# A four-layer graph network on one core: twenty mask pieces set earlier, and the first two weights of a unit made by the unit before it

## The chip, the cores and the metric

The kernel runs on one core of a Trainium2 chip. The metric is the device time of one execution in microseconds (us). The kernel before the change takes 3250.54 us, the median of three runs (3249.86 to 3252.36). Engines are called by their short names: PE (TensorE, matmuls; PEld is its loading of stationary operands), DVE (VectorE), ACT (ScalarE), POOL (GpSimd) and SP (SyncE, which here only issues transfers).

## The reference

The input is `x` (3327 x 512, float32) and an adjacency matrix `adj` (3327 x 3327, int32, zeros and ones). Four layers follow one another, and each is added to its input and normalised along the row:

```python
x = layernorm(x + gat(x, adj, W0, a0))            # layer 0, 8 heads
x = layernorm(x + sage(x, adj, ...))              # layer 1, first 64 neighbours of each row
x = layernorm(x + elu(gat(x, adj, W2, a2)))       # layer 2, 8 heads
x = layernorm(x + elu(gat(x, adj, W3, a3)))       # layer 3, 4 heads

def gat(x, adj, W, a):                            # per head
    h = x @ W
    e = leaky_relu((h @ a1)[:, None] + (h @ a2)[None, :], 0.2)
    return softmax(where(adj > 0, e, -9e15), axis=1) @ h
```

What matters here is that each attention layer needs, for every head, a 3327 x 3327 matrix of weights that are zero wherever `adj` is zero, and that the first layer has to read all of `adj` (4 bytes an element) before that is known on the chip.

## The kernel before

**Tiles and halves.** The rows are padded to 3328 = 26 tiles of 128 (`NT` = 26). A half of the rows is 13 tiles or 1664 columns (`HALF`, `IW`). The transposed adjacency matrix is turned once into a mask of ones and zeros in fp8, `mask0[p, t, i]`: tile `t` holds 128 neighbours, `i` runs over all 3328 rows. It is made in pieces `(t, q)`, `t` a tile and `q` a quarter of the columns (832): a load of int32 values, 416 KB, into a tile `raw` (L884, issued by SP), and a set, one instruction that compares it with zero, on DVE (L895) or on ACT (L894). Quarters 0 and 1 are the first half of the rows, 2 and 3 the second. That makes 104 pieces.

**The first projection** (the loop `for t in range(1, NT)` around L1443) takes one tile of `x` a turn: `project1` transposes it (PE L267, copy on ACT L268, a sum over it on DVE L269), `project2` of the tile before multiplies it by the weights (16 matmuls, PE L277) and scales the result on DVE (`vt`, L283), which POOL stores (L289). Two or three steps of `msteps` are written into each turn. A step `k` loads piece `k` and sets piece `k - 5`; there are eight `raw` tiles. Here the list has the 52 pieces of the first half. Late in the loop POOL also loads the row values of the first unit (`wide_rows`, `rba`, 2 x 832 KB).

**The attention of layers 0 and 2** (`attention8`, `unit8`) runs eight units of 26 tiles `j`. The units numbered 0 and 7 treat two heads over one half of the rows, and the six between treat one head over all rows. For each tile, DVE makes the weights `t` (L702, one pass over 3328 columns, or two over 1664), ACT turns them into the fp8 selector `y` (L703), and PE multiplies `t` with the values (L724, 16 instructions) and `y` with the pieces of the denominator (L680). There are three `t` tiles, so DVE can be up to three tiles ahead of PE. At the end of each turn one entry is taken from two lists: `background` (among it `count_jobs`, which on PE counts the mask's ones over all 26 tiles, L925) and `aside`. In layer 0 `aside` holds the other 52 mask pieces (`some`, four steps in three turns); here a step loads piece `k` and sets piece `k - 1`, there are two `raw` tiles, four in nine sets go to ACT, and each set is pinned.

**The attention of layer 3** (`attention`, `unit`) runs eight units as well: two halves of the rows by four heads `s`. For tile `j`, `weights(j, k)` issues the pass on DVE (L428) and the one on ACT (L431), PE multiplies (L451) and adds up the denominator (`den`, L403). At the end of a unit the four accumulators `po` are emptied into `ob`: in the first half by four DVE transposes (L470), in the second by a DVE copy (L474) and three ACT copies (L472). Where a denominator is complete, DVE also transposes it (L521, L525), reduces it (L529), and POOL spreads it over the partitions (L541). The next unit's first matmul must wait for `ob`, since it uses the same accumulators. `rows` (L372, POOL) loads the row values of a unit into one of two slots. In the second half of the rows, `aside` holds the finishing of the first half: loads, division by the denominator (L182), exponential (L189), sums (L197, L198), normalisation (L153 to L162) and stores.

**Order.** On PE the order is that of the program text (`tc.manual_schedule`). On the other engines a planner lays out each queue when the program is built: it plays the program through with its own durations, and an instruction that is ready in that play may stand ahead of earlier written ones. `tc.keep_in_program_order(ins)` ties an instruction behind the one written just before it on its engine ("pinned"). Each engine then works through its queue strictly in order, so one that waits holds up everything behind it.

Of the kernel before, what the change touches and what calls it, by code (L numbers as in the profile page):

```python
# [13 lines left out]
ALU = mybir.AluOpType  # L14
# [18 lines left out]
def kernel(  # L33
# [10 lines left out]
    nc = tc.nc  # L44
    N, F = x.shape
    NT = (N + P - 1) // P
# [3 lines left out]
    NS = F // P  # L50
    HALF = NT // 2
    FW = F // 2
    assert F == 512 and NT % 2 == 0 and N < NP and NT < 32
    IW = HALF * P
# [2 lines left out]
    CUTS = ((0, WA // 2), (WA // 2, WA), (WA, WA + WB // 2), (WA + WB // 2, IW))  # L57
    assert WA // 2 <= 512
    PIECES = (0, 48, 72, 32)
    QUADS = [(s, min(4, HALF - s)) for s in range(0, HALF, 4)]  # L60


# [55 lines left out]
    mask_at = []  # L118
# [113 lines left out]
    class Layer:  # L232
# [151 lines left out]
                                                                     u.half * IW:(u.half + 1) * IW].to_broadcast([P, IW]))  # L384
            return r_

        def unit(self, pools, half, s, background, aside, final=None, ending=None):
            H, D, HS = self.H, self.D, self.HS
            tp, yp, vp, rp, sp, po_p = pools
            i0 = half * IW  # L390
            heads = list(range(s * HS, (s + 1) * HS))
            rb, self.first_rows = self.first_rows or self.rows(rp, half, s), None
            po = [po_p.tile([P, 512], F32, name=f"po{c}") for c in range(4)]
            if s == 0:
                self.pd = [po_p.tile([P, 512], F32, name=f"pd{c}") for c in range(2)]
# [26 lines left out]
                       ys[j][k][:, a_:a_ + w_], w_,  # L422
                       s == NS - 1 or final is not None and s > 0)

            def weights(j, k):
                h = heads[k]
                t = tp.tile([P, IW], F32, name="t")
                nc.vector.scalar_tensor_tensor(t, rb[k], self.qc[:, j, h:h + 1],  # L428
                                               mask_at[0](j, i0, IW), op0=ALU.max, op1=ALU.mult)
                y = yp.tile([P, IW], F8, name="y")  # L430
                nc.scalar.activation(y, t, AF.Sigmoid, bias=self.bi[:, j, h:h + 1],  # L431
                                     scale=self.sc[:, j, h:h + 1], saturate=False)
                return t, y

            late = []
            for j in range(NT):
                if j % 2 == 0:
                    vj = vp.tile([P, 2, P], F32, name="vj")
                    nc.sync.dma_start(out=vj, in_=self.vd[j * P:(j + 2) * P, s * P:(s + 1) * P]
                                      .rearrange("(t p) f -> p t f", p=P))  # L440


                if HS == 1 or j not in (1, NT - 1):
                    made = {}
                    for k in range(HS):
                        for j_ in (j, j + 1) if HS > 1 and j in (0, NT - 2) else (j,):
                            made[j_, k] = weights(j_, k)
                ts, ys = zip(*(made[j, k] for k in range(HS)))
                for c, (a_, z) in enumerate(CUTS):
                    for k in range(HS):  # L450
                        nc.tensor.matmul(po[c][k * D:(k + 1) * D, :z - a_], vj[:, j % 2, k * D:(k + 1) * D],  # L451
                                         ts[k][:, a_:z], start=j == 0, stop=j == NT - 1)
                late.append(ys)
                if j % 4 == 0 and j > 0:
                    for j_ in (j - 4, j - 2):
                        den(j_, [late.pop(0), late.pop(0)])
                if background:
                    background.pop(0)()
                if aside:
                    aside.pop(0)()  # L460
            if ending:
                ending(sp)
            den(NT - 2, late)

            ob = sp.tile([P, IW], F32, name="ob", bufs=1)
            by_dma = HS == 1 and not final
            for c, (a_, z) in enumerate(CUTS):
                if by_dma:

                    nc.vector.transpose(ob[:, a_:z], po[c][:, :z - a_])  # L470
                elif c or HS == 2:
                    nc.scalar.copy(ob[:, a_:z], po[c][:, :z - a_])  # L472
                else:
                    nc.vector.tensor_copy(ob[:, a_:z], po[c][:, :z - a_])  # L474
            t0 = half * HALF

            def transposed(s0, n):
# [38 lines left out]
            if not by_pe:  # L516
# [2 lines left out]
                end = half == 1 and s == NS - 1  # L519
                for c in range(2):  # L520
                    ins = nc.vector.transpose(db[:64, c * (WA // 2):(c + 1) * (WA // 2)], pd[c][:64, :WA // 2])  # L521
                    if end and c == 0:

                        tc.keep_in_program_order(ins)
                    nc.vector.transpose(db[64:, c * (WB // 2):(c + 1) * (WB // 2)], pd[c][64:, :WB // 2])  # L525
                red = yp.tile([P, WA // 32, 2, NS], F32, name="red", tag="y")
                dv = db.rearrange("p (b s x) -> p b s x", s=NS, x=8)
# [88 lines left out]
        def attention(self, rp, extra=None, aside=(), later=None, final=None, ending=None):  # L616
            with tc.tile_pool(name="at_t", bufs=3 * self.HS, reuse_waits="tile") as tp, \
                    tc.tile_pool(name="at_y", bufs=7, reuse_waits="tile") as yp, \
                    tc.tile_pool(name="at_v", bufs=3, reuse_waits="tile") as vp, \
                    tc.tile_pool(name="at_s", bufs=2, reuse_waits="tile") as sp, \  # L620
                    tc.tile_pool(name="at_po", bufs=1, space=PSUM, reuse_waits="tile") as po_p:
                pools = (tp, yp, vp, rp, sp, po_p)
                jobs = []
                aside = list(aside)
                for half in range(2):
                    for s in range(NS):
                        if extra:
                            jobs += extra(sp, half, s)
                        if later and half == 1:
                            aside += later(s)  # L630
                        jobs += self.unit(pools, half, s, jobs, aside, final if half else None,
                                          ending if (half, s) == (1, NS - 1) else None)
                while jobs:
                    jobs.pop(0)()
                for f in aside:
                    f()
# [310 lines left out]
    class MaskTiles:  # L947
# [6 lines left out]
        def start(self):  # L954
            self.early = self.pools.enter_context(tc.tile_pool(name="mk_a", bufs=1, side="right", reuse_waits="tile"))
            self.tiles = {j: self.early.tile([P, NP], F8, name=f"mk{j}") for j in range(self.FIRST)}
# [435 lines left out]
    with tc.tile_pool(name="mask0", bufs=1, reuse_waits="tile") as mp0, \  # L1392
# [8 lines left out]
        with tc.tile_pool(name="p_w", bufs=1, reuse_waits="tile") as wp, \  # L1401
# [3 lines left out]
            if LAST < P:  # L1405
                nc.gpsimd.memset(mask0[:, NT - 1, :], 0.0)
            nc.gpsimd.memset(mask0[:, :, N:NP], 0.0)
            pieces = [(t, q, IW // 2) for t in range(NT) for q in range(2)]
            msteps = mask_steps(rw0, pieces, 5, (), False, 8)

            def load(t):
# [31 lines left out]
            for t in range(1, NT):  # L1443
                xT = L0.project1(pp, ps, load(t), t)
                L0.project2(pp, bank, wsb, *pend)
                pend = (xT, t)
                for _ in range(2 + (t % 3 == 1)):
                    if msteps:
                        msteps.pop(0)()
                if t == HALF + 1:  # L1450
                    L0.prepare(pp, 0)
                    L0.cut(pp, 0)
                if t == NT - 6:
                    L0.first_rows = L0.wide_rows(ring, UNITS[0])
# [22 lines left out]
            return []  # L1477


        pieces = [(t, q, IW // 2) for t in range(NT) for q in range(2, 4)]  # L1480
        rest = ExitStack()
        rawp = rest.enter_context(tc.tile_pool(name="raw", bufs=2))
        ring.insert(0, (rest.enter_context(tc.tile_pool(name="at_s0", bufs=1, reuse_waits="tile")), "rbb"))
# [86 lines left out]
```

## Time and profile before

| what | value |
| --- | --- |
| median of three runs | 3250.54 us |
| the profiled execution | 3248.35 us, of it the span of the engines' work 3246.5 us |
| PE busy | 3135.6 us (97%) |
| DVE, ACT busy | 2623.7 us (81%), 2293.6 us (71%) |
| first projection and what leads to it, to the first weights on DVE | 0 to 133.77 us |
| layer 0's attention, first to last of its matmuls' copies | 135.7 to 954.4 us |
| layer 3's attention, first matmul to last | 2555.9 to 3217.4 us |
| mask sets on DVE | 81, median 593 ns, the last at 319.4 us |
| mask sets on ACT | 23, median 988 ns, the last at 319.1 us |

PE is busy in nearly all of the span, so what counts is where PE stands still, or runs at less than its full clock, and what it then waits for. A timeline lists instructions in order of time: start, duration, engine, line, operation, tiles, and in brackets the idle time of that engine just before, with what ended it. The table of windows gives, for stretches of time, each engine's busy time with the number of instructions, the granted PE clock (1.00 is full), the DMA engines' share and what they moved.

### The profile page before, as it was taken

Reading aid. Unit: us, or ns where it says so; the run is one execution under the profiler, and the core shown is the slowest. Engines: PE = TensorE matmul, PEld = TensorE weight load, DVE = VectorE, ACT = ScalarE, POOL = GpSimd, SP = SyncE. Lnnn points to the kernel's source line nnn. Section 1 sums busy time; section 2 is a strip of 40 time slices with the busy share of each in tenths; the row PEclk is TensorE's granted clock in tenths of the full one; section 3 lists DMA queues with packets and bytes.
Section 4 is the critical chain, followed back from the end, with each engine's and each line's share of the span. In section 5 each row is a group of like instructions: output and inputs, shape, how many; then the busy total and the mean of one; then the engine's idle time right before and its main releaser. Section 6 shows DMA issues by size and latency. Waiting matters only on the chain. (4 is left out here: it accounts for less than half of the span.)

```text
span 3246.5 us, 44851 instructions
## 1 busy us (share of the span) xinstructions
PE 3135.6 (97%) x17910; PEld 1599.6 (49%) x17910; DVE 2623.7 (81%) x2320; ACT 2293.6 (71%) x1826; POOL 231.8 (7%) x378
## 2 busy tenths in 40 slices
PE   8998999999999999999989999999988999999997
PEld 7643343333334467777733333333337655555453
DVE  5698999999987645555499999999989666677887
ACT  2498888899873334444388988899988655568886
POOL 3100000000010111111100000000001000010110
PEclk9999999999999999999999999999999999999998
DMA  9554114111134345555331111011137211122211
GB/s 366 171 175 145 41 52 145 51 42 41 29 99 131 99 134 130 139 141 146 105 122 55 41 35 41 21 41 42 28 100 238 96 42 43 44 56 89 88 42 52
DMA packets 354575, 300.07 MB, mean 92 GB/s; under 512 B 232420, under 2 KB 288174, under 8 KB 352831
## 3 DMA queue, kind: packets, MB, share of 16 engines
q1 hardware_dynamic: 322175, 185.92, 19.9%
q0 software_dynamic: 26672, 103.60, 10.2%
q10 hardware_dynamic: 5520, 7.69, 0.7%
q8 instruction: 141, 2.31, 0.3%
q14 instruction: 67, 0.55, 0.1%
HBM read 220.27 MB, written 76.84 MB: 92 GB/s over the span
## 5 line engine op out<-in xcount | busy, mean ns | idle before, releaser
L703 ACT ACTIVATE y<-t,bi,sc 128x3328 fp8e4<-128x3328 f32 (+1 forms) x520 | 1337.3, 2603 | 109.2 <-DVE t L702 51.4
L724 PE MATMUL po<-t,vj 128*64 128x448 f32 (+1 forms) x6656 | 1278.4, 525 | 16.6 <-DVE t L702 15.6
L724 PEld LDWEIGHTS po<-t,vj 128*64 128x64 f32 x6656 | 459.0, 138 | 703.4 <-issue 632.3
L451 PE MATMUL po<-t,vj 128*128 128x448 f32 (+1 forms) x1664 | 599.4, 517 | 5.6 <-DVE t L428 3.5
L428 DVE SCALAR_TENSOR_TENSOR t<-rba,qc,mk 128x1664 f32<-128x1664 f32 x208 | 404.1, 1947 | 141.2 <-PE po L451 109.6
L431 ACT ACTIVATE y<-t,bi,sc 128x1664 fp8e4<-128x1664 f32 x208 | 365.6, 1772 | 184.4 <-DVE t L428 167.7
L451 PEld LDWEIGHTS po<-t,vj 128*128 128x128 f32 x1664 | 311.5, 190 | 274.1 <-issue 170.9
L702 DVE SCALAR_TENSOR_TENSOR t<-rba,qc,mk 128x3328 f32<-128x3328 f32 (+1 forms) x130 | 379.6, 2986 | 11.8 <-DMA mk<-md 7.8
L702 DVE SCALAR_TENSOR_TENSOR t<-rbb,qc,mask 128x3328 f32<-128x3328 f32 (+1 forms) x130 | 380.3, 2981 | 9.1 <-PE po L724 6.2
L702 DVE SCALAR_TENSOR_TENSOR t<-rbb,qc,mk 128x3328 f32<-128x3328 f32 (+1 forms) x130 | 379.2, 2985 | 8.7 <-PE po L724 6.7
L702 DVE SCALAR_TENSOR_TENSOR t<-rba,qc,mask 128x3328 f32<-128x3328 f32 (+1 forms) x130 | 380.5, 2981 | 6.7 <-PE po L724 5.9
L1164 PE MATMUL acc<-zs,kt 128*128 128x512 f32 x1352 | 360.2, 420 | 0.0
L277 PE MATMUL pw<-wsb,xT 128*128 128x264 f32 (+1 forms) x1248 | 297.7, 393 | 6.3 <-DVE vt L283 3.5
L1164 PEld LDWEIGHTS acc<-zs,kt 128*128 128x128 f32 x1352 | 255.6, 189 | 52.1 <-PE pk L1015 0.8
L680 PE MATMUL pd<-y,sden 128*32 128x384 fp8e4 (+1 forms) x3328 | 271.2, 344 | 0.0
L277 PEld LDWEIGHTS pw<-wsb,xT 128*128 128x128 f32 x1248 | 238.9, 195 | 49.2 <-ACT xT L268 5.2
L1022 ACT CAST pk<-cy 128x512 f32<-128x512 bf16 x169 | 99.1, 587 | 222.4 <-DVE kt L1036 215.9
L1036 DVE SCALAR_TENSOR_TENSOR kt<-pk,mb 128x512 fp32r<-128x512 f32 x169 | 115.4, 684 | 116.7 <-PE pk L1033 115.5
L680 PEld LDWEIGHTS <-sden 128*32 128x32 bf16 x3328 | 89.5, 95 | 165.8 <-issue 150.2
L283 DVE TENSOR_TENSOR vt<-pw,dc 128x256 f32<-128x256 f32 x156 | 59.1, 418 | 90.6 <-ACT dc L278 84.6
L1062 PE MATMUL pz<-wn,xT 128*128 128x512 f32 x208 | 96.0, 605 | 6.1 <-DMA wn<-in_wnT_dram 5.4
L992 POOL DMA_DIRECT2D cy<-ctd x91 | 67.9, 746 | 366.9 <-ACT pk L1022 301.2
(221 smaller groups left out, 2079.3 us busy)
## 6 DMA issues: line engine op xcount, KB each, us to landing
raw<-in_adjT_dram SPq DMA_DIRECT2D x67, 416.0 KB
vj<-v SPq DMA_DIRECT2D x156, 128.0 KB
cy<-ctd POOLq DMA_DIRECT2D x78, 256.0 KB, 4.3
h<-hd SPq DMA_DIRECT2D x61, 256.0 KB
v<-vt SPq DMA_DIRECT2D x50, 256.0 KB
xr<-x POOLq DMA_DIRECT2D x45, 256.0 KB, 3.4
md<-mask SPq DMA_DIRECT2D x26, 416.0 KB
mb<-md SPq DMA_DIRECT2D x169, 64.0 KB
```

The source lines that it names most:

```text
L277: nc.tensor.matmul(pw[e][:, :FW + H], xT[:, c, :], wsb[:, c, e, :], start=c == 0, stop=c == FC - 1)
L428: nc.vector.scalar_tensor_tensor(t, rb[k], self.qc[:, j, h:h + 1], mask_at[0](j, i0, IW), op0=ALU.max, op1=ALU.mult)
L431: nc.scalar.activation(y, t, AF.Sigmoid, bias=self.bi[:, j, h:h + 1], scale=self.sc[:, j, h:h + 1], saturate=False)
L451: nc.tensor.matmul(po[c][k * D:(k + 1) * D, :z - a_], vj[:, j % 2, k * D:(k + 1) * D], ts[k][:, a_:z], start=j == 0, stop=j == NT - 1)
L680: nc.tensor.matmul(pd[c][32 * kk:32 * kk + 32, :w_], lhsT, rhs, start=(kk, c) not in seen, stop=last and j == NT - 1)
L702: nc.vector.scalar_tensor_tensor(to, ro, self.qc[:, j, h:h + 1], m, op0=ALU.max, op1=ALU.mult)
L703: nc.scalar.activation(yo, to, AF.Sigmoid, bias=self.bi[:, j, h:h + 1], scale=self.sc[:, j, h:h + 1], saturate=False)
L724: nc.tensor.matmul(po[c][k * D:(k + 1) * D, :z - a_], vj[:, j % 2, x_:x_ + D], t[:, k, a_:z], start=j == 0, stop=j == NT - 1)
L1022: nc.scalar.copy(pks[k % 2], carry[b, t // 4 * 4][:, t % 4:t % 4 + 2, :])
L1036: nc.vector.scalar_tensor_tensor(kt, pk, NEIGHBOURS, mb[:, t:t + 2, :], op0=ALU.is_le, op1=ALU.mult)
L1062: nc.tensor.matmul(pz, xT[:, c, :], wn[:, c, :], start=c == 0, stop=c == FC - 1)
L1164: nc.tensor.matmul(acc, kts[b, t][:, s * P:(s + 1) * P], zs(t, c), start=t == 0 and c == 0, stop=t == NT - 1 and c == 1)
```

## The change

It has two parts. First, the ten tiles 0 to 9 of the second half of the rows (`EARLY` = 10, quarters 2 and 3, twenty pieces) move from layer 0's attention to the end of the projection's list. That list grows from 52 to 72 pieces, and its steps from 57 to 77; the turns 22 to 25 of the projection now hold seven steps each in place of two or three. The list in the attention shrinks from 52 to 32 pieces (33 steps in place of 53); at four steps in three turns it ends in unit 0, where before it ran on into unit 1.

Second, in layer 3 a unit knows its follower (`following`). At tile 13 it loads the follower's row values. After its last tile it makes the follower's weights of tile 0 (`start(0)`), and, after emptying the accumulators, those of tile 1 (`start(1)`); both DVE passes are pinned. The follower takes them from `self.started`. All transposes of the first part of the denominator on DVE are pinned now, where only one was.

```diff
+    EARLY = 10
...
-            def weights(j, k):
-                h = heads[k]
+            def weights(j, k, rb=rb, h0=heads[0], i0=i0, pinned=False):
+                h = h0 + k
                 t = tp.tile([P, IW], F32, name="t")
-                nc.vector.scalar_tensor_tensor(t, rb[k], self.qc[:, j, h:h + 1],
-                                               mask_at[0](j, i0, IW), op0=ALU.max, op1=ALU.mult)
+                ins = nc.vector.scalar_tensor_tensor(t, rb[k], self.qc[:, j, h:h + 1],
+                                                     mask_at[0](j, i0, IW), op0=ALU.max, op1=ALU.mult)
+                if pinned:
+                    tc.keep_in_program_order(ins)
...
+                ts, ys = zip(*([started.pop(j)] if j in started else [weights(j, k) for k in range(HS)]))
+                if following and j == HALF:
+                    self.first_rows = self.rows(rp, *following)
...
             if ending:
                 ending(sp)
+
+            def start(j):
+                if following:
+                    self.started[j] = weights(j, 0, self.first_rows, following[1], following[0] * IW, True)
+
+            start(0)
             den(NT - 2, late)
 
             ob = sp.tile([P, IW], F32, name="ob", bufs=1)
...
                 else:
                     nc.vector.tensor_copy(ob[:, a_:z], po[c][:, :z - a_])
+            start(1)
             t0 = half * HALF
...
                     ins = nc.vector.transpose(db[:64, c * (WA // 2):(c + 1) * (WA // 2)], pd[c][:64, :WA // 2])
-                    if end and c == 0:
-
-                        tc.keep_in_program_order(ins)
+                    tc.keep_in_program_order(ins)
...
-            pieces = [(t, q, IW // 2) for t in range(NT) for q in range(2)]
+            pieces = [(t, q, IW // 2) for t in range(NT) for q in range(2)] + \
+                [(t, q, IW // 2) for t in range(EARLY) for q in range(2, 4)]
             msteps = mask_steps(rw0, pieces, 5, (), False, 8)
...
                 pend = (xT, t)
-                for _ in range(2 + (t % 3 == 1)):
+                for _ in range(2 + (t % 3 == 1) if t < NT - 4 else 7):
                     if msteps:
                         msteps.pop(0)()
...
-        pieces = [(t, q, IW // 2) for t in range(NT) for q in range(2, 4)]
+        pieces = [(t, q, IW // 2) for t in range(EARLY, NT) for q in range(2, 4)]
```

## The prediction, made before the change was run

> **What bounds the kernel now.** I read the page's busy shares first: PE 97%, DVE 81%, ACT 71%. The kernel can gain only where PE stands still or runs slowly, so the next view was PE's timeline, searched for idle times above 0.25 us, and then the DVE's and ACT's timelines at those places. The chain that ended last covers only the tail after 3138 us and says nothing on these stages.
>
> The stage that loses mask sets is layer 0's unit 1, some 254 to 371 us. PE, then DVE, then ACT:
>
> ```profile
> 254.41 3.16 PE L724 MATMUL po<-t,vj 128*64 128x448 f32 x16
> 260.48 4.71 PE L724 MATMUL po<-t,vj 128*64 128x448 f32 x16 [2.91 <-DVE t L702]
> 310.78 3.02 PE L724 MATMUL po<-t,vj 128*64 128x448 f32 x16 [0.82 <-DVE t L702]
> 320.10 0.59 PE L925 MATMUL pct<-mask,onecol 128*32 128x512 fp8e4 x1 [4.15 <-ACT mask L894]
> 320.61 5.66 PE L724 MATMUL po<-t,vj 128*64 128x448 f32 x16
> ...
> 256.24 0.60 DVE L895 TENSOR_SCALAR mask<-raw 128x831 fp8e4<-128x831 int32 x1 [4.29 <-DMA raw<-in_adjT_dram]
> ...
> 319.07 0.97 ACT L894 ACTIVATE mask<-raw,below 127x832 fp8e4<-127x832 int32 x1
> ```
>
> Three idle times of PE come from mask pieces. The set at 256.24 waits 4.29 us for its load and holds up the weights behind it; 0.82 us goes the same way; at 320.10 the count over all 26 tiles waits 4.15 us for the last set. After the long ones the same 16 matmuls take 4.71 and 5.66 us where 3.01 is usual.
>
> The stage that takes over the twenty pieces:
>
> ```profile
> 69.98 3.80 PE L277 MATMUL pw<-wsb,xT 128*128 128x264 f32 x16 [0.20 <-DVE vt L283]
> 74.42 3.80 PE L277 MATMUL pw<-wsb,xT 128*128 128x264 f32 x16 [0.20 <-DVE vt L283]
> ...
> 118.43 3.73 PE L277 MATMUL pw<-wsb,xT 128*128 128x264 f32 x16
> ...
> 60.00:70.00 10.00, 9.42 (x48) 7.54 (x46) 6.99 (x15) 2.54 (x12) 2.15 (x4) 1.00 1.03 407
> ...
> 110.00:120.00 10.00, 10.00 (x53) 8.64 (x52) 4.33 (x9) 2.79 (x11) 1.62 (x3) 1.00 0.14 53
> ```
>
> Up to 95 us, where the last of the 52 sets runs, transfers fill the DMA engines (407 GB/s) and a tile takes 4.43 us, with three sets on DVE in it; after that PE sets a pace of 4.00 us, and DMA and DVE have room.
>
> The stage of the second part, layer 3, is full of PE at seven boundaries of units but for two:
>
> ```profile
> 2967.57 0.69 DVE L182 TENSOR_TENSOR h<-h,rec 128x512 f32<-128x512 f32 x1 [4.10 <-DMA h<-hd]
> 2968.29 0.62 DVE L474 COPY ob<-po 128x448 f32<-128x448 f32 x1
> 2968.97 8.65 PE L451 MATMUL po<-t,vj 128*128 128x448 f32 x24 [2.08 <-DVE ob L474]
> ...
> 3051.08 0.62 DVE L521 STREAM_TRANSPOSE db<-pd 64x448 f32<-64x448 f32 x1
> 3051.72 0.59 DVE L525 STREAM_TRANSPOSE db<-pd 64x384 f32<-64x384 f32 x1
> 3056.59 10.34 PE L451 MATMUL po<-t,vj 128*128 128x448 f32 x24 [3.51 <-DVE t L428]
> ```
>
> At 2966.9 us the copy that frees an accumulator stands behind a division whose load is late. At 3053.1 us the second weight of the new unit is made only after the denominator's transposes.
>
> **What the Trainium skill says.** "TensorE: Matmul & The Clock Gate", part 1, "What's actually happening": after an idle window of about 3.4 us the array's clock falls to half, and about as long of work brings it back. The windows agree: granted clock 0.50 from 320.6 to 323.0 us and 0.59 from 260.5 to 264.0; even the 2.91 us gap brought it on, while those of 0.82 and 1.23 us were followed by matmuls of the usual length. "DMA: Bandwidth & Descriptors", "Where 436 GB/s comes from": a ceiling of 435 GB/s, with the memory's share of about 358 binding first. Here the plateau is 405 to 411 GB/s, so the measurement decides. "Perfetto Trace Analysis", "Identifying the Most-Contended Engine": matmul busy time is no measure of PE's room[...]. The 97% agrees with that: it includes the slow matmuls above.
>
> **Part one, what it removes.** The list of 33 steps ends in turn 24 of unit 0, as four steps go in three turns. Unit 0 keeps the same density of sets, so nothing changes there. In unit 1 all sets go: the three gaps, 2.91 + 0.82 + 4.15 = 7.88 us, and the slow matmuls after them, (4.71 - 3.01) + (5.66 - 3.01) = 4.35 us; together 12.2 us. What is late next? DVE makes 3328 columns in 3.59 us from start to start. Without the wait, tile 1's weights are ready at 251.9 + 3.6 = 255.5 us, and PE wants them at 257.6. Over the unit DVE needs 26 x 3.59 = 93.3 us and about 6 for small operations. PE needs 26 x 3.43, plus 9 x 0.37 for the mask's share of the denominator, 7.3 for counts, 3.0 for sums and 2.2 for transposes, 105 in all. So PE stays the bound. In units 2 to 6 PE is busy without gaps, so the gain is kept. I take -12 us (-8 if the slow clock stays or DVE is late somewhere, -12.5 at best).
>
> **Part one, what it adds.** Twenty loads of 416 KB (8.5 MB), issued by SP, and twenty sets of 0.58 us on DVE, 11.6 us, in the eight tiles from 95 to 130 us. A tile's own work there is 0.76 + 0.69 us of DVE, so 2.5 of each 4.0 us are free: 20 us for 11.6. The planner let the first 52 pieces run seven tiles ahead of where they are written (the last set, of turn 25, stands at tile 17), so I expect it to spread these twenty from tile 18 on. DMA is tighter. From 95 us it has to move 8.5 MB of mask, 2.0 of `vt`, 0.8 of `x` and most of the 1.7 of row values: 12.8 MB, at 405 GB/s 31.6 us. That fits into the 38 us up to the first weights, but not evenly: with three pieces a tile the twenty take 6.7 tiles, which carry about 12.5 MB and so 30.9 us where PE needs 26.8, +4 us. Each set that waits for its load holds `vt` back behind it on DVE, and with it PE and POOL's store. Loads that SP issues for the attention (`vj`) are now behind mask loads, but are first used at 135 us. Bounds: 0, if two or three a tile just fit; +8 if five a tile fall into the last four turns (2.39 MB, 5.9 us against 4.0, four times). I take +3.5.
>
> **Part two.** PE's order is unchanged, and the same 208 passes are made. Before, at most boundaries DVE had already made both first weights ahead (at 2798.33 us the second one, 2.8 us before PE ended the unit). After, the second is pinned behind the emptying of the accumulators. Boundary by boundary: the three within the first half stay without a gap, since the second weight comes at about 2804.5 us in the old time and is wanted at 2805.5. At 2882 us DVE now has the second weight (1.9) ahead of the transposes (2.5); the third weight is done at about 2888.7, or 2889.7 behind the reduction, and wanted at 2888.2: +0.5 to +1.5 us. At 2966.9 us the copy may or may not still stand behind the division: 0 to -2.1, I take -1. At 3053.1 us the second weight comes in time, but the transposes (2.5), the reduction and statistics (2.5) then delay the third to as late as 3058.8 where PE wants it at 3056.2. Of 3.51 us plus 1.2 of slow matmuls (10.34 - 3 x 3.06) between 1 and 4.7 goes; I take -2. The last boundary stays without a gap: its third weight is ready long before 3142.8. The row values came some 80 us early in the first half (POOL waits 79 us for a slot and then loads them at 2875), and need the same slot as before. Together -2 us, between -7 and +2.
>
> **Sum.** -12 + 3.5 - 2 = -10.5 us. Against the profiled execution, 3248.35 us, of which 1.85 lies outside the span, that is 3237.9. The median of the runs lies 2.2 us above it, and I give the forecast on the median's scale: 3240.
>
> **The rivals.** A: the projection gives most of it back. DMA at 407 GB/s speaks for it, the room on DVE and DMA after 105 us against it. With +8 there and nothing in layer 3: -12 + 8 = -4, 3246.5. B: layer 3's two gaps go whole. The pin behind the copy speaks for the first, the DVE's load (20 of 25 us) against the second: -12 + 3.5 - 7 = -15.5, 3235. C, slower: mask sets in DVE's queue for which the loads are late stop the tile work from 95 us on, so that loads and PE's work follow one another in place of lying side by side. Price: 8.5 MB at 405 GB/s = 21 us, so -12 + 21 - 2 = +7, 3257.5. It decides once the projection ends more than 14 us later. Against it stands that up to 95 us three pieces cost a tile 0.43 us, not 3. D: the change doesn't do what it says, because sets still end late in unit 1. Pinned as they are, they follow the turns, and turn 24 of unit 0 is the last; I give it no weight of its own.
>
> **Chances.** Forecast 0.64, A 0.16, B 0.10, C 0.10. The difference that a measurement of this kernel can tell from none is about 0.2%, 6.5 us. Faster by more: nearly all of the forecast, B, and a little of A, 0.70. Within: most of A and the weak edge of the forecast, 0.19. Slower: C, 0.11. The range 3231 to 3252 takes in both parts at their best (-12.5 - 7), B, the forecast and A; C and the last tenth stay out.
>
> **What would show it.** Right: the sets in the second list end before about 245 us; the count in unit 1 has no wait; the matmuls of unit 1 stay at 3.01 us; the time from the unit's first to its last tile falls by about 12 us; tiles in the projection take about 4.4 us from 95 to 125 us. Wrong: a projection that ends after 144 us, or new gaps before layer 3's third weights larger than those removed. The forecast fails upward if the planner stacks the twenty sets, downward if DMA hides them all and both gaps in layer 3 close.

## The result and the profile after

The changed kernel takes 3250.27 us, the median of 12 runs (3244.22 to 3257.87); the kernel before, run beside it, 3250.68 us (12 runs, 3245.86 to 3254.26). The ratio is 1.0000 with a 95% interval of 0.9991 to 1.0009: no difference. The forecast was 3240, ten microseconds less. The profiled execution took 3250.52 us with a span of 3248.8, 2.3 us more than the span before.

The busy shares of the changed kernel (us, share of the span, instructions):

```profile
PE 3139.2 (97%) x17910; PEld 1601.2 (49%) x17910; DVE 2627.8 (81%) x2329; ACT 2286.6 (70%) x1817; POOL 233.5 (7%) x378
```

It looks like the page before. Two effects of opposite sign lie under it, and only the timelines show them. The timeline of the changed kernel in unit 1 of layer 0 (start, duration, engine, line, operation, tiles, idle time before):

```profile
256.63 3.02 PE L731 MATMUL po<-t,vj 128*64 128x448 f32 x16
...
261.20 5.81 PE L731 MATMUL po<-t,vj 128*64 128x448 f32 x32
...
325.69 1.73 PE L932 MATMUL pct<-mask,onecol 128*32 128x512 fp8e4 x26
327.35 3.02 PE L731 MATMUL po<-t,vj 128*64 128x448 f32 x16
...
254.55 0.59 DVE L902 TENSOR_SCALAR mask<-raw 127x831 fp8e4<-127x831 int32 x1
```

The last mask set is at 254.55 us, where before sets ran on to 319. The count over 26 tiles runs through without a wait, and 32 matmuls take 5.81 us: the three idle times and the slow matmuls after two of them are gone. From its first matmul to the next unit's, unit 1 takes 105.40 us in place of 116.79. The projection, in the timeline of the same kernel (PE, then DVE):

```profile
103.68 2.61 PE L278 MATMUL pw<-wsb,xT 128*128 128x264 f32 x11
...
109.39 5.49 PE L278 MATMUL pw<-wsb,xT 128*128 128x264 f32 x16 [2.67 <-DVE vt L284]
...
116.35 3.80 PE L278 MATMUL pw<-wsb,xT 128*128 128x264 f32 x16 [1.03 <-DVE vt L284]
...
106.15 0.59 DVE L902 TENSOR_SCALAR mask<-raw 128x832 fp8e4<-128x832 int32 x1 [2.15 <-DMA raw<-in_adjT_dram]
108.32 0.59 DVE L902 TENSOR_SCALAR mask<-raw 128x831 fp8e4<-128x831 int32 x1 [1.58 <-DMA raw<-in_adjT_dram]
108.83 0.75 DVE L284 TENSOR_TENSOR vt<-pw,dc 128x256 f32<-128x256 f32 x2
...
140.05 3.73 DVE L709 SCALAR_TENSOR_TENSOR t<-rba,qc,mask 128x1664 f32<-128x1664 f32 x2
```

PE stands 2.67 us for `vt`. On DVE `vt` (108.83) stands behind two mask sets that wait for their loads. The 16 matmuls after the gap take 5.49 us where 3.73 to 3.80 is usual. The first weights come at 140.05 us, 6.3 later than before. The table of windows of the changed kernel (window; busy time with instructions of PE, PEld, DVE, ACT, POOL; granted clock; share of the DMA engines; GB/s) shows why the loads are late:

```profile
100.00:110.00 10.00, 7.33 (x38) 6.12 (x37) 4.40 (x9) 1.97 (x8) 1.75 (x4) 1.00 1.02 407
110.00:120.00 10.00, 8.97 (x36) 7.14 (x35) 5.79 (x12) 1.15 (x5) 1.78 (x3) 0.83 1.03 387
```

The DMA engines are full from 100 to 120 us, where before they moved 251 and 53 GB/s. Layer 3, in the timeline of the changed kernel (DVE and PE at the boundaries of the units at about 2966, 3050 and 3137 us, and ACT at the last of them):

```profile
2964.21 0.69 DVE L183 TENSOR_TENSOR h<-h,rec 128x512 f32<-128x512 f32 x1 [7.07 <-DMA h<-hd]
2964.93 0.62 DVE L481 COPY ob<-po 128x448 f32<-128x448 f32 x1
2965.61 6.76 PE L452 MATMUL po<-t,vj 128*128 128x448 f32 x13 [2.19 <-DVE ob L481]
...
3045.06 1.29 DVE L198 SCALAR_TENSOR_TENSOR xr<-e,xr 128x512 f32<-128x512 f32 x2 [2.86 <-ACT e L190]
3046.27 1.29 DVE L199 SCALAR_TENSOR_TENSOR h<-h,xr 128x512 f32<-128x512 f32 x2
3047.47 1.94 DVE L430 SCALAR_TENSOR_TENSOR t<-rba,qc,mk 128x1664 f32<-128x1664 f32 x1
3049.34 0.62 DVE L481 COPY ob<-po 128x448 f32<-128x448 f32 x1
3049.87 1.94 DVE L430 SCALAR_TENSOR_TENSOR t<-rba,qc,mk 128x1664 f32<-128x1664 f32 x1
...
3050.01 5.86 PE L452 MATMUL po<-t,vj 128*128 128x448 f32 x16 [1.41 <-DVE ob L481]
3058.38 5.88 PE L452 MATMUL po<-t,vj 128*128 128x448 f32 x11 [2.52 <-DVE t L430]
...
3133.80 0.43 DVE L1321 SCALAR_TENSOR_TENSOR xr<-e,xr 128x256 f32<-128x256 f32 x1 [4.65 <-ACT e L1316]
3134.60 1.95 DVE L430 SCALAR_TENSOR_TENSOR t<-rba,qc,mk 128x1664 f32<-128x1664 f32 x1
...
3136.90 0.54 PE L405 MATMUL pd<-y,sden 128*32 128x448 fp8e4 x6 [1.42 <-ACT y L435]
...
3132.05 1.28 ACT L1316 ACT_TABLE_LOAD   x1
3133.35 0.42 ACT L1316 ACTIVATE e<-g 128x256 f32<-128x256 f32 x1
3133.78 1.28 ACT L435 ACT_TABLE_LOAD   x1
3135.08 3.44 ACT L435 ACTIVATE y<-t,bi,sc 128x1664 fp8e4<-128x1664 f32 x2
3138.42 1.27 ACT L479 COPY ob<-po 128x448 f32<-128x448 f32 x3
```

The copy at 2964.93 still stands behind the division. At 3047.47 and 3134.60 the follower's first weight comes only after sums that wait for ACT's exponential (2.86 and 4.65 us). At 3050 the copy that frees the accumulator stands behind that weight, and PE waits for it. At 3137 PE waits for something else: for the selector of the old unit's last tile, in the denominator. Of the two selectors at 3135.08 the first is the old unit's last; on ACT it stands behind an exponential and two loads of tables. The second is the follower's first, and the copies at 3138.42 that free the other accumulators stand behind it. Layer 3 had two gaps of PE, 2.08 and 3.51 us. It now has six: 0.63 (at 2884.33, third weight), 2.19, 1.41, 2.52, 1.42 and 0.59 us.

The balance of the two profiled executions, from the starts of the same instructions (tile 17 of the projection, counted from 0, is where the first of the twenty pieces are set; its first matmul is that of L277 before and L278 after):

| stage | before | after | difference |
| --- | --- | --- | --- |
| to the first matmul of tile 17 | 94.43 | 94.57 | +0.1 |
| from there to the first weights of layer 0 on DVE (133.77, 140.05) | 39.34 | 45.48 | +6.1 |
| from there to the gap ahead of layer 0's last weights (946.61, 941.44) | 812.84 | 801.39 | -11.5 |
| from there to layer 3's first matmul (2555.93, 2551.45) | 1609.3 | 1610.0 | +0.7 |
| layer 3, first matmul to last (3216.96, 3218.46) | 661.0 | 667.0 | +6.0 |
| from there to the end of the span | 29.5 | 30.3 | +0.8 |

One trace is one execution, and the stages do not repeat equally well. In all the traces below, the one from tile 17 to the first weights takes 39.33 or 39.34 us in the seven kernels with the old list of pieces, and layer 3 takes 660.4 to 661.2 us in the four in which it is as before. These two stages can be compared to the microsecond. The start of the projection is looser: in the seven kernels the first weights come anywhere from 133.77 to 136.15 us. From the first to the last weights of layer 0 these seven take 812.8 to 817.6 us, and from there to layer 3 all kernels take 1603.9 to 1612.7, although no edit is written into that stretch; why is not explained here. So medians and intervals carry the verdicts on the time, and the two firm stages carry the readings of what each edit costs.

### The profile page after: what moved, and what is told of

It reads as the page before. It is cut to its first block, busy times and chain, and to the rows that moved or that the text cites. A ratio compares the mean times of both kernels' runs of the same rounds, so it can differ in the third digit from the quotient of the medians.

```text
span 3248.8 us, 44852 instructions
## 1 busy us (share of the span) xinstructions
PE 3139.2 (97%) x17910; PEld 1601.2 (49%) x17910; DVE 2627.8 (81%) x2329; ACT 2286.6 (70%) x1817; POOL 233.5 (7%) x378
## 4 chain that ended last, share of the span: by engine, by line
PE 81%; DVE 6%; issue 4%; DMA 4%; ACT 3%; POOL 0%; SPq 0%; POOLq 0%; DVEq 0%; ACTq 0%
PE po L731 35%; PE po L452 13%; PE acc L1171 9%; PE pd L687 7%; PE pw L278 6%; DVE t L709 3%; PE pz L1069 3%; PE pi L1072 3%; DMA raw<-in_adjT_dram 2%; PE pd L405 1%; PE pk L1040 1%; ACT y L435 1%; PE pt L751 1%; DVE t L430 1%; PE pe L793 1%
## 5 line engine op out<-in xcount | busy, mean ns | idle before, releaser
L278 PE MATMUL pw<-wsb,xT 128*128 128x264 f32 (+1 forms) x1248 | 299.3, 395 | 10.3 <-DVE vt L284 8.2
L278 PEld LDWEIGHTS pw<-wsb,xT 128*128 128x128 f32 x1248 | 239.9, 196 | 53.2 <-ACT xT L269 6.2
```

What stands on the lines that cost most here:

```text
L278: nc.tensor.matmul(pw[e][:, :FW + H], xT[:, c, :], wsb[:, c, e, :], start=c == 0, stop=c == FC - 1)
```

## The experiments

The theory after reading: part one gains about what was forecast, less a stall in the projection where the row load of the first unit lies among the mask loads; part two loses, because a pinned weight is put behind finishing work that waits. Rivals: the projection pays for the number of pieces; the pinned pass costs by its place alone; in layer 3 ACT is the bound whatever is pinned. The ratios are to the kernel before in the same set of runs, whose median was 3250.09 (44 runs), 3250.23 (30) and 3250.04 us (31).

**Each part alone.** The first kernel has the hunks of the diff around `EARLY`, the second all the others.

> Only the mask part of the change; layer 3 as before. Theory (the two parts have opposite signs): the first weights come some 6 us later than before (140 against 133.8 us), unit 1 of layer 0 is 12 us shorter, so the kernel is about 5 us faster than before, 3245. Rival (the mask part gives everything back by itself, for example in layer 2, where the changed kernel's lead shrank from 6.8 to 4.6 us): within 1 us of before, 3250.

> Only the layer 3 part of the change; mask as before. Theory (opposite signs): about 6 us slower than before, 3256.5, with all of it between the second half of layer 3's first unit and the end: idle times of PE of about 1.4 us at two places of the third boundary's and the fourth boundary's kind that before didn't have. Rival (layer 3 is neutral): 3250, and the last matmul as far from the first of layer 3 as before (661.5 us).

| kernel | median us (range, runs) | ratio (95%) | tile 17 to first weights (before 39.3) | layer 3 (before 661.0) |
| --- | --- | --- | --- | --- |
| part one alone | 3241.17 (3237.57 to 3244.41, 6) | 0.9975 (0.9963 to 0.9986) | 45.2 | 661.2 |
| part two alone | 3258.85 (3252.6 to 3262.6, 7) | 1.0026 (1.0014 to 1.0038) | 39.3 | 666.4 |

By medians, -8.9 and +8.8 us: they add up to -0.1 where the whole change has -0.4. Each is uncertain by some 4 us, so that they match so closely is chance; but both intervals leave out 1. That the time did not move is a sum of two real effects. Of part two's loss the trace finds 5.4 us in layer 3, which the interval allows (4.6 to 12.4).

**Part two with its pins taken away.** In the first kernel the follower's first weight is free for the planner, in the second both are (the last argument is `False`).

```diff
-                    self.started[j] = weights(j, 0, self.first_rows, following[1], following[0] * IW, True)
+                    self.started[j] = weights(j, 0, self.first_rows, following[1], following[0] * IW, j == 1)
```

> As part2_alone, but the pass of start(0) isn't pinned, so that the planner may put it ahead of the finishing work of the unit's last turn; start(1) and the transposes stay pinned. Theory (the pin of the first weight puts it behind a sum that waits for ACT's exponential): the gap before PE's last denominator matmuls of the boundary at 3137 us and the 1.4 us one at 3050 us are gone, 2 to 4 us faster than part2_alone. Rival (the pin of the second weight and the transposes behind it cost the time): within 1 us of part2_alone.

> As part2_alone, but neither of the two weights is pinned; the transposes stay pinned. Theory (pins on the weights cost the time): back to before's 3250 or up to 2 us better, since a unit's second weight may again be made ahead of the emptying of the accumulators. Rival (it is the place in the text, ahead of other work in the planner's play, or the pinned transposes, not the pins on the weights): within 2 us of part2_alone.

Measured: 3253.77 us (21 runs; ratio 1.0016, 1.0010 to 1.0023) and layer 3 of 663.3 us with the first weight free; 3252.65 us (21 runs; 1.0006, 0.9999 to 1.0013) and 661.6 us with both free. In time the intervals of part two alone and with the first weight free overlap, so the reading rests on layer 3. Its units 0 to 3 take 326.3 to 326.4 us in every kernel; the others, each from its first matmul to the next unit's, the last to its own last (us):

| kernel | unit 4 | unit 5 | unit 6 | unit 7 |
| --- | --- | --- | --- | --- |
| before | 86.77 | 81.05 | 86.71 | 80.22 |
| the whole change | 87.77 | 84.39 | 87.36 | 81.09 |
| part two alone | 87.47 | 84.21 | 87.33 | 81.09 |
| first weight free | 87.43 | 81.22 | 87.25 | 81.09 |
| both free | 86.82 | 81.03 | 86.34 | 81.09 |
| both free, no switch of tables (below) | 86.74 | 81.04 | 83.91 | 80.23 |

The pin of the first weight goes with some 3 us, all in unit 5: 1.4 is the wait for the copy at its end, the rest slow matmuls at its start, behind the gap at 2966. The two kernels of the table with that pin show them and the others do not, after gaps of much the same length; that the pin is their cause is not shown. The pin of the second weight goes with 1.7 us: some 0.6 in unit 4, where the gap of 0.63 us goes, and 0.9 in unit 6, where slow matmuls go and the wait at its end grows. Against what was expected, the wait in the denominator at the last boundary is still 1.41 us with the first weight free and 2.09 with both: no pin on a weight causes it. And without these pins the part still gains nothing: layer 3 is back where it was, and no gain appears. Unit 6 takes 86.3 to 87.4 us in the first five kernels, whatever stands at its start. Its end, in the timeline of the kernel with both free (ACT, then PE):

```profile
3133.47 1.28 ACT L1315 ACT_TABLE_LOAD   x1
3134.77 0.63 ACT L1315 ACTIVATE e<-g 128x512 f32<-128x512 f32 x1
3135.42 1.28 ACT L434 ACT_TABLE_LOAD   x1
3136.71 3.44 ACT L434 ACTIVATE y<-t,bi,sc 128x1664 fp8e4<-128x1664 f32 x2
...
3145.01 0.54 PE L404 MATMUL pd<-y,sden 128*32 128x448 fp8e4 x6 [2.09 <-ACT y L434]
```

ACT has no idle time here. For two selectors it spends 1.28 + 0.63 + 1.28 + 3.44 = 6.63 us, since a table is loaded ahead of the exponential of the finishing work and again ahead of the sigmoid. Two tiles cost PE 6.13 us in all, the denominator with them (79.70 us for the 26 tiles of each of the units 1 to 3). So PE catches up with ACT within the unit. The pins on the transposes stayed in all these runs and were not tested alone.

**The same without the switch of tables.** To see whether ACT is that bound, the exponential in `first_slots` is computed as a sigmoid; all else is the kernel with both free. This kernel leaves out the exponential and computes something else; it serves only to measure.

```diff
-                        nc.scalar.activation(e[:, :n], y, AF.Exp)
+                        nc.scalar.activation(e[:, :n], y, AF.Sigmoid)
```

> As part2_free_both, but the exponential of layer 3's fourteen slot sums is computed with the sigmoid in its place (seven instructions, results differ), so that ACT has no change of tables in the unit before the last, 18 us of table loads less. Theory (in that unit ACT has become the bound, so that what PE gains at the boundary at 3050 us it loses at the one at 3137 us): the wait of the last denominator matmuls for ACT (2.09 us) and that for the emptied accumulator (0.59 us) there go, layer 3 from first to last matmul takes 659 us in place of 661.6. Rival (the wait there comes from the order of the weights and copies on ACT alone): the waits stay within 0.5 us, 661.6.

Measured: 3248.46 us (14 runs; ratio 0.9995, 0.9986 to 1.0005; in time not to be told from the kernel with both free), layer 3 of 658.2 us, 3.4 less than with the switches: 2.4 in unit 6 and 0.9 in unit 7. PE's timeline of this kernel at the same boundary:

```profile
3131.01 3.06 PE L451 MATMUL po<-t,vj 128*128 128x448 f32 x8
3134.00 0.56 PE L404 MATMUL pd<-y,sden 128*32 128x448 fp8e4 x8
3134.49 14.23 PE L451 MATMUL po<-t,vj 128*128 128x448 f32 x40
```

No gap is left there, so the switches did bound that stretch: what PE gained at the start of unit 6 it lost at its end, waiting for ACT. The Trainium skill, "ScalarE: Activation LUTs", "What ACT_TABLE_LOAD costs", gives about 1283 ns for a load, which the trace has too (1.28 us), and adds a drain of about 1380 ns to every switch; no such time shows here, as the exponential starts 1.30 us after its load starts, and the load at 3133.47 us starts as the selector before it ends.

**The row load behind the mask loads.** Part one alone, with the two loads of `rba` issued by POOL in turn 24 in place of turn 20, and pinned there (the pin stands in `wide_rows`, not shown).

```diff
-                if t == NT - 6:
-                    L0.first_rows = L0.wide_rows(ring, UNITS[0])
+                if t == NT - 2:
+                    L0.first_rows = L0.wide_rows(ring, UNITS[0], True)
```

> As part1_alone, but the load of the first unit's row values (2 x 832 KB, POOL) is moved to turn 24 of the projection and pinned there, behind the mask loads. Theory (the 6 us that the projection gained come from that load falling together with the mask loads: three sets in a row then wait some 2 us each and PE stands for 2.95 and 1.93 us at 109 and 115 us): these two gaps fall below 1 us together, the first weights come at about 136 us, the kernel is 3 to 5 us faster than part1_alone, 3237. Rival (it is the bytes, not when they fall: 1 us of DMA a piece): the gaps move to another tile, first weights at 140 us as before, within 1.5 us of part1_alone.

Measured: 3237.18 us (8 runs; ratio 0.9964, 0.9953 to 0.9976), first weights at 135.52 us, 40.6 after tile 17. In time the interval overlaps that of part one alone; the stage decides. The timeline of this kernel, PE and then DVE, where part one alone had gaps of 2.95 and 1.93 us:

```profile
106.93 3.73 PE L278 MATMUL pw<-wsb,xT 128*128 128x264 f32 x16
...
111.16 3.80 PE L278 MATMUL pw<-wsb,xT 128*128 128x264 f32 x16
...
115.53 3.80 PE L278 MATMUL pw<-wsb,xT 128*128 128x264 f32 x16
...
135.52 5.60 DVE L705 SCALAR_TENSOR_TENSOR t<-rba,qc,mask 128x1664 f32<-128x1664 f32 x3
```

From tile 17 on, the same twenty pieces now cost 1.3 us (1.9 in the kernel with both edits below) in place of 5.0 to 6.1 in three traces, and the gaps have not moved elsewhere (one of 0.34 us is left), although the DMA engines are as full from 100 to 120 us (399 GB/s, with 407 and 387 in the changed kernel). The rows (1.7 MB, 4.2 us at 405 GB/s) were first used at 139 us but loaded from 92 us on.

**Ten pieces in place of twenty.** Part one alone with `EARLY = 5`.

> As part1_alone, but ten pieces move in place of twenty (EARLY 5). The list in the attention then has 43 steps and ends in turn 6 of unit 1. Theory (each piece costs the projection about 0.3 us, and unit 1 has two separate costs, one at its start of 2.9 + 1.7 us and one at the count of 4.15 + 2.65 + 0.8): the first weights come at about 136 us, the count has no wait, the gap at the start of unit 1 stays, so the kernel is within 2 us of part1_alone, some 5 us faster than before. Rival (the loss in the projection starts only with the last pieces): first weights at 134 us, 2 us faster than part1_alone.

Measured: 3247.42 us (13 runs; ratio 0.9993, 0.9985 to 1.0001). The timeline of PE:

```profile
111.82 3.80 PE L278 MATMUL pw<-wsb,xT 128*128 128x264 f32 x16 [3.14 <-DVE vt L284]
...
116.98 3.80 PE L278 MATMUL pw<-wsb,xT 128*128 128x264 f32 x16 [0.93 <-DVE vt L284]
...
267.37 4.55 PE L725 MATMUL po<-t,vj 128*64 128x448 f32 x16 [2.98 <-DVE t L703]
```

The expectation of a gain of some 5 us was missed. Half the pieces cost the projection 4.5 us from tile 17 on, where the twenty cost 5.0 to 6.1; the first weights at 140.40 us also reflect a later start of tile 17 (96.53 us). So its price is not one per piece. And the gain is cut: the list in the attention now ends within unit 1, the count's wait is gone, but the gap at the unit's start stays.

**The finishing work six turns later.** In layer 3 the list `aside` begins with 12 empty turns in the second half; 18 move the whole finishing work, and with it the loads and waits that had stood at the boundaries. First on top of part one, then on the kernel before, then on part two with both its pins.

```diff
-                        jobs += [none] * 12
+                        jobs += [none] * 18
```

> As part1_alone, but the finishing work of layer 3's second half starts six turns later (18 empty jobs ahead of it in place of 12), so that no division with a late load stands ahead of the copy that empties the accumulator at a unit's end. Theory (the two gaps of layer 3 come from finishing work that falls on the boundaries): the gap of 2.1 us at 2963 us goes, the one of 3.5 us at 3050 falls below 1.5, layer 3 takes 657 us in place of 661.2 and the kernel is 3 to 5 us faster than part1_alone, 3237. Rival (ACT bounds the unit before the last, and late finishing work makes that worse): the first gap goes, but the last two units get longer by as much; within 1.5 us of part1_alone.

> The kernel before with 18 empty turns in place of 12 ahead of the finishing of layer 3, and nothing else. If the finishing work at the boundaries is what costs layer 3 its gaps in the kernel before too, the two gaps at 2969 and 3057 us (2.08 and 3.51 us) go and layer 3 takes 656 us in place of 661: 3250 - 4 = 3246 us. If the gain belongs to part one's other timing, layer 3 stays at 661 us and the time at 3250.

> Part two alone with 18 empty turns in place of 12 ahead of the finishing of layer 3. If the pinned weights lose by standing behind finishing work that waits for ACT, then moving that work away from some boundaries takes back part of the loss at each boundary it leaves: layer 3 falls from 666 to about 660 us, the time from 3259 to 3252. If the pin costs by its place alone, the gaps of PE at the second half's boundaries stay as they are, layer 3 at 666 us and the time at 3259.

| kernel | median us (range, runs) | ratio (95%) | layer 3 | layer 3 with 12 |
| --- | --- | --- | --- | --- |
| part one, 18 | 3237.07 (3233.94 to 3243.07, 5) | 0.9966 (0.9954 to 0.9978) | 655.8 | 661.2 |
| before, 18 | 3243.90 (3237.97 to 3249.42, 18) | 0.9983 (0.9976 to 0.9991) | 655.8 | 661.0 |
| part two, 18 | 3243.05 (3237.81 to 3248.25, 14) | 0.9978 (0.9970 to 0.9986) | 656.8 | 666.4 |

If the pins cost by their place alone, layer 3 would have stayed at 666 us. Part two with all its pins loses little once the finishing work stands elsewhere: 3258.85 falls to 3243.05 us, which cannot be told from the kernel before with the same 18 turns, and in layer 3 0.9 us of the loss is left. The move takes the loads, the sums and the exponentials along together, so this run does not separate the wait on DVE from the one on ACT. It has a price too: in the kernel before with 18 turns the two gaps are gone, but one of 2.19 us comes at the last boundary (unit 7 takes 82.68 us in place of 80.22). Two boundaries show the gain. The timeline of part one with 18 turns, DVE and PE, where the kernel before had 2.08 us:

```profile
2957.24 0.62 DVE L475 COPY ob<-po 128x448 f32<-128x448 f32 x1 [0.56 <-PE po L452]
2959.82 1.48 DVE L183 TENSOR_TENSOR h<-h,rec 128x512 f32<-128x512 f32 x2 [1.96 <-DMA h<-hd]
...
2960.04 6.23 PE L452 MATMUL po<-t,vj 128*128 128x448 f32 x17
```

The copy now stands ahead of the division that waits for `h`. And the timeline of part two with 18 turns, where the whole change had the waits of 2.86, 1.41 and 2.52 us:

```profile
3043.52 1.95 DVE L429 SCALAR_TENSOR_TENSOR t<-rba,qc,mk 128x1664 f32<-128x1664 f32 x1
3045.39 0.62 DVE L480 COPY ob<-po 128x448 f32<-128x448 f32 x1
3045.92 1.94 DVE L429 SCALAR_TENSOR_TENSOR t<-rba,qc,mk 128x1664 f32<-128x1664 f32 x1
...
3050.30 1.95 DVE L429 SCALAR_TENSOR_TENSOR t<-rba,qc,mk 128x1664 f32<-128x1664 f32 x1
...
3049.12 9.94 PE L451 MATMUL po<-t,vj 128*128 128x384 f32 x28 [0.91 <-ACT ob L478]
```

The first three follow one another at once, the third weight is ready at 3052.25, and one gap of 0.91 us remains at this boundary.

**All of it together.** Part one with the row load late and 18 empty turns, with twenty and with 26 pieces (`EARLY = 13`).

> Part one, with the row load of unit 1 of layer 0 issued behind turn 24 of the projection, and with the finishing of the first half of layer 3 given 18 empty turns in place of 12. If the row load and the finishing are two separate costs, both gains come on top of part one's: 3241 - 4 - 4 = 3233 us, ratio 0.9946, first weights of layer 0 on DVE at 135.5 us and layer 3 of 656 us from first to last matmul. If one of the two gains was drift of the middle of the kernel and not its own, the time stays at 3237.

> As the first of these, with 26 early pieces in place of 20. If pieces cost the projection nothing once the row load is out of the way, first weights stay at about 136 us and the time at 3233. If the transfers are then full again, each piece costs its 416 KB at 405 GB/s, 1.03 us: six of them +6 us, first weights at 141 to 142 and 3239 us.

Measured: 3234.80 us (5 runs, 3228.3 to 3241.3; ratio 0.9953, 0.9940 to 0.9967) and 3233.69 us (5 runs, 3231.78 to 3241.42; 0.9956, 0.9943 to 0.9969). Both are faster than the two kernels studied, by about 0.45%; they cannot be told from each other. In the stages both gains are there: 41.3 us from tile 17 to the first weights, where part one alone has 45.2, and layer 3 of 655.7 us. In time they are not: with five runs the step from 0.9966 to 0.9953 is within the intervals, and in this trace unit 1 of layer 0 takes 107.08 us where part one alone takes 103.75. In the kernel with 26 pieces the six more cost the projection 1.1 us (42.4 from tile 17), of which 0.97 is a wait of the first weights for the rows themselves: there the row load can't go later. The whole change with the late row load and 18 turns was not run; part two adds nothing in its own test, so about the same time would be expected.

## Why the prediction failed where it did

**Part one, what it removes: right.** Forecast -12 us, in the trace -11.5 from the first weights to the last of layer 0's, and -11.4 in unit 1 alone. The count does not wait. The sets end at 254.55 us and not before 245 as said, 6.3 us of that because the layer starts later; they still end ahead of unit 1. What was late next was nothing, as the sum of PE's and DVE's loads had it. That the matmuls stay at 3.02 us is true but for one tile: the 16 matmuls at 274.46 us take 4.42, with no gap ahead of them (last section). Where that tile too runs at its usual length, as in part one alone, unit 1 takes 103.75 us.

**Part one, what it adds: the right mechanism, mis-sized.** The term was +3.5, the trace has +6.1 from tile 17 on (part one alone +5.9). The step took 12.5 MB over 6.7 tiles as an even flow at 405 GB/s. The flow was even at 407 and 387 GB/s, but what it carried was not: after the 1.7 MB of row values had shared it, the mask loads came late one after another, DVE stood in its queue, and two tiles took most of the loss, 2.67 + 1.03 us of gaps and 1.7 us of slow matmuls (5.49 - 3.80). The other tiles kept a pace of about 4.0 us, where 4.4 had been named as the sign. The text listed the row load in the sum and did not ask when it was needed; moved to its need, the term becomes +1.3. That it should have been priced per piece is refuted by the ten pieces. Rival A had +8 for this term and was a little nearer on it; rival C, in which loads and PE's work follow one another, is refuted.

**Part two: the step that failed.** The forecast was -2 us, between -7 and +2; layer 3 took +6.0, and part two alone cost +8.8 by medians. By units the +6.0 is 0.1 up to unit 4, then 1.0, 3.3, 0.7 and 0.9. The step made three assumptions that do not hold.

First, it took the pin of the second weight as the one that matters and worked out where that weight comes; the first weight, pinned too, was not followed in the queue. It stands behind whatever the program writes before it, and in the second half of layer 3 that is finishing work which waits for ACT. At 3050 us this costs the 1.41 us for the copy behind that weight. Before, the planner had laid the weight ahead of the sums, in the timeline of the kernel before:

```profile
3044.17 1.94 DVE L428 SCALAR_TENSOR_TENSOR t<-rba,qc,mk 128x1664 f32<-128x1664 f32 x1
...
3046.94 1.29 DVE L197 SCALAR_TENSOR_TENSOR xr<-e,xr 128x512 f32<-128x512 f32 x2 [0.82 <-ACT e L189]
```

Second, it set ACT at nothing. The gain of 1 to 4.7 us that it saw at 3053 can't be kept while the exponentials of the finishing work fill ACT up to the end of unit 6, where it needs 6.63 us for two selectors with an exponential between them and two tiles cost PE 6.13: the unit took 0.7 us more, not 2 less, with the weights free it gained 0.4, and without the switches 2.8. Third, it said that the last boundary stays without a gap because its third weight is early. PE waited there 1.42 us for the old unit's last selector and 0.59 us for copies behind the follower's first selector; that selector is written ahead of the copies now, pinned or not, and with 12 empty turns both waits went only with the switches of tables. The remaining gain, at 2966, did not come, since the copy stayed behind the division (2.19 us); 1.9 us of slow matmuls followed that gap, which the 2.08 us before had not brought. The 0.63 us at 2884 was forecast (+0.5 to +1.5).

That the time still lies within 3231 to 3252 is luck as far as part two goes: the range reached that far for rival A's sake, and A expected nothing from layer 3. The reason of A was half of the truth: the projection did give back more than forecast, but without part two the kernel gains 0.25%.

What stays open: the drift between traces in stages that no part touches, why the gap at 2966 is followed by slow matmuls in some kernels, and whether the time keeps the whole of the late row load's gain beside the other edit.

## What to carry to other kernels

A pin does not only place an instruction, it can place it behind a wait: before pinning something early on the path, read what is written just ahead of it on its engine and what that waits for. Then ask which engine is next: a gap of PE that closes is no gain where another engine, here ACT with its tables, sets the pace of the whole unit. Work that has time, such as finishing work or a load that is needed only some 45 us later, cost little here by its length but much by its place: moving both was worth 6.4 us by medians on top of the 8.9 of part one, with intervals that just overlap. When a change of two parts moves nothing, run the parts alone first: here -8.9 and +8.8 us stood behind a ratio of 1.0000.

## What the hardware showed beside that

A short idle time of PE is not always followed by slow matmuls. The 16 matmuls of a projection tile take 3.73 to 3.80 us. After 2.67 us of idle they took 5.49 in the changed kernel, with a granted clock of 0.64 from 111.0 to 114.5 us; after 3.14 us they took 3.80 with ten pieces, and after 2.95 us 3.80 with part one alone. Nor is idle time needed. In layer 0's unit 1 of the changed kernel, 26 narrow matmuls come without a gap ahead of a tile:

```profile
271.23 3.31 PE L793 MATMUL pe<-c,db 128*128 128x16 f32 x26
274.46 4.42 PE L731 MATMUL po<-t,vj 128*64 128x448 f32 x16
```

The granted clock is 0.50 from 274 to 277 us, and the tile takes 4.42 us where 3.02 is usual. In part one alone the same tile behind the same narrow matmuls takes 3.02 us. "TensorE: Matmul & The Clock Gate", part 1, "What's actually happening", in the Trainium skill, has the clock fall after at least one idle window of about 3.4 us, and calls the window free-running. The shorter gaps here do not fit the first as it stands; the second would explain why equal gaps end differently, but no run here shows the phase of the window. In practice the price of such a gap in the projection is the gap, or the gap and some 1.7 us, and these traces give no way to tell ahead.
